# A cross-attention kernel on one core: query weights kept in DRAM, values loaded for two quads, and some transfers issued by GpSimd

## The chip, the cores and the metric

One of the eight cores of a Trainium2 chip runs the kernel. The metric is device time in microseconds (us). The engines are TensorE (PE in the profile, its weight loads PEld), VectorE (DVE), ScalarE (ACT), GpSimd (POOL) and SyncE (SP). In the kernel before, SyncE issues all transfers but two small ones of ScalarE, which load gamma and beta.

## The reference

```python
mu  = jnp.mean(hidden_states, axis=-1, keepdims=True)
var = jnp.var(hidden_states, axis=-1, keepdims=True)
x = (hidden_states - mu) * jax.lax.rsqrt(var + LN_EPS) * ln_gamma + ln_beta
Q = _split_heads(x @ Wq.T)                # 32 heads of 32
K = _split_heads(memory_keys); V = _split_heads(memory_values)
scores = jnp.einsum('bhsd,bhtd->bhst', Q, K) * scale
probs = jax.nn.softmax(jnp.where(mask, scores, -jnp.inf), axis=-1)
attn = jnp.einsum('bhst,bhtd->bhsd', probs, V)     # back to (B, S, 1024)
out = residual + attn @ Wout.T
```

There are 8 batches, 256 queries and 256 keys each, 1024 features, all in fp32. Keys and values are the same input, ctx_4096.

## The kernel before, in words

The unit of work is a quad: four heads of one batch. There are 64 quads, eight to a batch, and the main loop (line 926) has one slot for each, n = 0 to 63. The order of the instructions on each engine is written out by hand, there is no scheduler, and each engine takes its instructions strictly in that order. A wait at the head of a queue holds everything behind it.

In slot n TensorE does: the scores of quad n+1 (`scores`, line 486), the product of the probabilities of quad n-2 with its values (`values`, line 629), a share of a query projection (`make_q`, line 345, for the first three batches; `query_product`, line 447, after that), and some steps of the output projection of the batch before (`product_steps`, line 715). At which place of the slot these steps stand is a table of three counts for each slot of a batch: place 0 is behind the scores, place 1 behind the values, place 2 at the slot's end (`STEPS`, line 662). The program's matmul on fp32 shows as two rows of the trace.

The other engines do the softmax of quad n+1 in slot n (`softmax_parts`). For each head VectorE adds the mask and takes the extreme (line 522), ScalarE takes the exponential with its sum (526), VectorE inverts the sum (533), GpSimd multiplies by it (535, `normalize`), VectorE transposes 32x32 blocks into the tile `pT` (541), and ScalarE copies half of it aside into `pc` (547). Then the tail of the quad: two transfers move parts of `pT` inside `pT` (607), two more bring `pc` into `pT` (611), the second pair waiting for the first to land. For quads below 8, and for those near the end, the tail is put off into the next slot, behind its first exponentials. `ahead` are loads that stand in front of the tail, `between` are loads between its two pairs of transfers.

Both projections use Strassen-Winograd products from batch 3 on (queries) and in the output projection (the last batch has an order of its own), seven products in place of eight. They need sums of weight blocks: B11, B12, B21, B22 are the quarters, T1 to T4 sums of them. GpSimd forms them in slots 3 to 14 for the output weights (`sum_wo`, line 185) and in slots 9 to 22 for the query weights (`sum_wq`, line 398). Before that GpSimd multiplies gamma into the query weights (`fold`, line 366), one of eight chunks at the end of each of the slots 0 to 7. The query sums do not all fit in the on-chip memory: T1 and T3 lie in DRAM (`kept`), and each batch loads them in turn into one tile, `ring` (`load_ring`, line 414); B11 and T4 stay on the chip. The query tile of TensorE has one PSUM buffer of the pool `ps_q`, which ScalarE (`copy_q`, lines 352 to 358) has to empty before TensorE starts the next query product.

The inputs of a batch go through a layer norm: `load_x`, then statistics and the norm (lines 231 to 257), VectorE's block transposes (316), and sixteen small transfers (`move_x`, line 332), which stand in SyncE's queue as four, six and six behind the tails of three slots. The values of a quad are loaded by `load_v` (line 144) in slot n, for use in slot n+2, into one of two buffers of a quad each. The output of a batch is added to the residual by VectorE and GpSimd and stored by SyncE (`store`, line 758, right behind VectorE's addition; `send`, line 744).

Of the kernel before, what the change touches and what calls it, by code (L numbers as in the profile page):

```python
# [46 lines left out]
F32 = mybir.dt.float32  # L47
# [12 lines left out]
def xattn_kernel(  # L60
# [30 lines left out]
    rp = ctx.enter_context(tc.tile_pool(name="rp", bufs=4))  # L91
    lnp = ctx.enter_context(tc.tile_pool(name="lnp", bufs=2))
    kp = ctx.enter_context(tc.tile_pool(name="kp", bufs=2))
    vp = ctx.enter_context(tc.tile_pool(name="vp", bufs=2))
    atp = ctx.enter_context(tc.tile_pool(name="atp", bufs=3))
    ep = ctx.enter_context(tc.tile_pool(name="ep", bufs=4))
    ptp = ctx.enter_context(tc.tile_pool(name="ptp", bufs=3))
    asp = ctx.enter_context(tc.tile_pool(name="asp", bufs=2))
# [24 lines left out]
    xs, ks, vs, rs = {}, {}, {}, {}  # L123

    def load_x(b, s, h=None):

        if b not in xs:
            xs[b] = xp.tile([P, NS, D], F32, tag="x", name=f"x_{b}")
        cols = ds(0, D) if h is None else ts(h, 512)
        nc.sync.dma_start(xs[b][:, s, cols], x[b, ts(s, P), cols])  # L130

    def load_k(n):
# [3 lines left out]
        nc.sync.dma_start(  # L136
            ks[n], kv[b, g // 2, :, : 2 * T].rearrange("p (g t) -> p g t", g=2)
        )

    def load_v(n):  # L140

        b, g = divmod(n, NQ)
        vs[n] = vp.tile([P, NI, P], F32, tag="v", name=f"v_{n}")
        nc.sync.dma_start(
            vs[n],
            kv[b, g // 2, :, ds(2 * T + n % 2 * NI * P, NI * P)].rearrange("p (i v) -> p i v", i=NI),
        )

    def load_res(b, s, h):
        rs[b, s, h] = rp.tile([P, 512], F32, tag="r", name=f"r_{b}_{s}_{h}")  # L150
        nc.sync.dma_start(rs[b, s, h], x[b, ts(s, P), ts(h, 512)])
# [9 lines left out]
        for name in ("T1", "T3")  # L161
    }
    w_t4 = const.tile([P, NK, NK, P], F32, tag="t4", name="t4")
# [7 lines left out]
    def load_wo(which, pair):  # L171
# [3 lines left out]
        nc.sync.dma_start(  # L175
            wo[:, which, ts(pair, 2)], rows.rearrange("(c p) q -> p c q", c=2)
        )

    def sum_wo(which, c):
# [5 lines left out]
        nc.gpsimd.tensor_tensor(wo[:, which, c], wo[:, a, c], wo[:, b, c], op)  # L185
# [24 lines left out]
    load_v(1)  # L210
    for o in range(5, 8):
        load_wq(o)
    for which, pair in ((B12, 0), (B22, 0), (B11, 0), (B12, 1), (B22, 1), (B11, 1)):
        load_wo(which, pair)
# [106 lines left out]
    def move_x(b, part):  # L321
# [8 lines left out]
        for i in part:  # L330
            a, q = i % NA, (i + i // NA) % NA
            nc.sync.dma_start(to_move[b][ts(q, K), a], xes[b][ts(a, K), q])
# [31 lines left out]
    def fold(o):  # L364

        nc.gpsimd.tensor_tensor(
# [11 lines left out]
    SPLIT = 3  # L378
    SOON, LATE = 0, NK
    W_AT = {"B12": (SOON, 0), "B22": (SOON, NK), "B11": (LATE, 0), "B21": (LATE, NK),  # L380
            "T2": (SOON, 0), "T3": (SOON, 0)}

    def weights(name, o):
# [3 lines left out]
        if name == "T4":  # L387
            return w_t4[:, o]
# [3 lines left out]
    def sum_wq(to, o):  # L392
# [5 lines left out]
        nc.gpsimd.tensor_tensor(weights(to, o), weights(a, o), weights(b, o), op)  # L398
# [739 lines left out]
```

## Time and profile before

| what | value |
|---|---|
| time, three runs | 577.17, 577.49, 578.33 us; median 577.49 us |
| profiled execution, first to last instruction (its span) | 577.0 us; no other time is recorded for it |
| the median over that span | 0.49 us |
| TensorE busy, matmuls | 567.3 us, 98% |
| VectorE, ScalarE, GpSimd busy | 460.4, 411.7, 409.8 us (80%, 71%, 71%) |
| DMA traffic | 111.69 MB, mean 194 GB/s |

A row of a timeline or of the groups names line, engine and operation, then the tile written and the tiles read. "Idle before" in brackets is time that the engine stood still just before the row, and what ended it. A row of SPq is the issuing of a transfer by SyncE, not the transfer. PEclk is the TensorE clock granted, as a share of full speed.

### The profile page before, as it was taken

How to read it: one execution, taken by the hardware profiler on the slowest of the kernel's cores; microseconds unless marked ns; L12 is line 12 of the kernel's file. 1: busy time of each engine (PE TensorE's matmuls, PEld its weight loads, DVE VectorE, ACT ScalarE, POOL GpSimd, SP SyncE). 2: the span in 40 equal slices, each digit the busy share in tenths (PEclk: the TensorE clock that was granted, in tenths of full speed). 3: DMA queues.
4: the chain of work that ended last, by engine and by line, in shares of the span. 5: the costliest groups of instructions: out<-in, count | busy, mean ns of one | idle time of the engine just before them, and what ended most of it. 6: DMA issues, size and time to landing. Idle time of an engine off the chain costs nothing. (4 is left out here: it accounts for less than half of the span.)

```text
span 577.0 us, 20128 instructions
## 1 busy us (share of the span) xinstructions
PE 567.3 (98%) x7162; PEld 394.2 (68%) x7162; DVE 460.4 (80%) x1695; ACT 411.7 (71%) x1425; POOL 409.8 (71%) x677
## 2 busy tenths in 40 slices
PE   8999998999999999999999999999999999999997
PEld 8788784667667777677676677667766767755543
DVE  5888887788877879979888788988878878779823
ACT  4697886677667877688677867768767776769810
POOL 1778898889896896876568675676658657448770
PEclk9999999899999999999999999999999999999999
DMA  8974766656677777957678856687567864446751
GB/s 304 394 206 126 208 161 180 192 148 166 185 220 222 200 208 207 271 166 201 188 213 228 211 138 189 212 240 206 148 161 236 224 170 130 130 138 178 199 166 73
DMA packets 50100, 111.69 MB, mean 194 GB/s; under 512 B 9424, under 2 KB 10192, under 8 KB 50000
## 3 DMA queue, kind: packets, MB, share of 16 engines
q1 hardware_dynamic: 49712, 110.40, 66.8%
q8 instruction: 57, 0.93, 0.7%
q14 instruction: 43, 0.35, 0.2%
q10 hardware_dynamic: 288, 0.01, 0.0%
HBM read 60.04 MB, written 10.49 MB: 122 GB/s over the span
## 5 line engine op out<-in xcount | busy, mean ns | idle before, releaser
L535 POOL TENSOR_SCALAR e<-e,rden 128x256 f32<-128x256 f32 x512 | 236.0, 478 | 116.9 <-DVE rden L533 114.4
L526 ACT ACTIVATE e<-e,mn 128x256 f32<-128x256 f32 x512 | 253.9, 501 | 50.7 <-DVE mn L522 49.6
L541 DVE STREAM_TRANSPOSE pT<-e 128x512 f32<-128x512 f32 x256 | 180.9, 707 | 44.7 <-POOL e L535 32.7
L522 DVE CUSTOM_DVE_ANT_0 e<-sc,mb 128x256 f32<-128x256 f32 x512 | 185.4, 416 | 26.4 <-PE sc L486 26.0
L547 ACT COPY pc<-pT 128x512 f32<-128x512 f32 x128 | 79.0, 617 | 72.1 <-DVE pT L541 36.6
L526 ACT ACTIVATION_READ_ACCUMULATOR e<-e,mn 128x1 f32 x512 | 97.9, 191 | 0.0
L345 PE MATMUL pq<-xnT,wq 128*128 128x256 f32 (+1 forms) x368 | 84.1, 383 | 0.6 <-ACT qa L354 0.6
L345 PEld LDWEIGHTS pq<-xnT,wq 128*128 128x128 f32 x368 | 68.9, 190 | 15.4 <-issue 3.7
L629 PE MATMUL pv<-pT,v 64*32 64x128 f32 x4096 | 74.7, 274 | 3.5 <-DMA v<-in_kv_dram 2.9
L629 PEld LDWEIGHTS pv<-pT,v 64*32 64x32 f32 x4096 | 57.5, 105 | 26.7 <-issue 14.7
L486 PEld LDWEIGHTS sc<-k,qa 32*128 32x128 f32 x1024 | 46.2, 184 | 41.9 <-issue 23.6
L715 PE MATMUL po_S<-wo,at 128*128 128x512 f32 x152 | 74.3, 606 | 0.0
L486 PE MATMUL sc<-k,qa 32*128 32x256 f32 x1024 | 73.6, 401 | 0.1
L715 PE MATMUL po_A<-wo,at 128*128 128x512 f32 x128 | 61.2, 620 | 0.3 <-ACT qa L354 0.3
L715 PE MATMUL po_S<-wo,s 128*128 128x512 f32 x104 | 49.9, 606 | 0.0
L533 DVE RECIPROCAL rden<-den 128x2 f32<-128x2 f32 x256 | 37.6, 147 | 7.7 <-ACT e L526 6.8
L522 DVE DVE_READ_ACCUMULATOR2_ANT mn<- 128x1 f32 x512 | 42.5, 83 | 0.0
L715 PEld LDWEIGHTS po_A<-wo,at 128*128 128x128 f32 x128 | 23.4, 193 | 26.2 <-issue 24.5
L447 PEld LDWEIGHTS pq_A<-xnT,wq 128*128 128x128 f32 x320 | 37.3, 192 | 4.8 <-issue 3.6
L715 PEld LDWEIGHTS po_S<-wo,at 128*128 128x128 f32 x152 | 25.8, 190 | 19.7 <-issue 19.1
L447 PE MATMUL pq_A<-xnT,wq 128*128 128x128 f32 x320 | 37.3, 275 | 0.0
L748 POOL TENSOR_TENSOR r<-r,p 128x512 f32<-128x512 f32 x23 | 29.4, 1278 | 7.1 <-DMA r<-in_x_dram 3.3
(96 smaller groups left out, 608.7 us busy)
## 6 DMA issues: line engine op xcount, KB each, us to landing
v<-in_kv_dram SPq DMA_DIRECT2D x64, 256.0 KB, 3.9
pT<-pT SPq DMA_DIRECT2D x128, 128.0 KB, 3.1
pT<-pc SPq DMA_DIRECT2D x128, 128.0 KB, 3.5
ring<-kept_T SPq DMA_DIRECT2D x18, 512.0 KB, 5.2
k<-in_kv_dram SPq DMA_DIRECT2D x32, 256.0 KB, 3.1
x<-in_x_dram SPq DMA_DIRECT2D x14, 512.0 KB, 5.1
r<-in_x_dram SPq DMA_DIRECT2D x28, 256.0 KB, 5.1
out_dram<-r SPq DMA_DIRECT2D x28, 256.0 KB, 3.0
```

The costliest lines, as they stand in the source:

```text
L345: nc.tensor.matmul(pqs[n], wq[:, o, c, :], xnTs[b](c), start=(c == 0), stop=(c == NC - 1),)
L447: nc.tensor.matmul(pqs[b][:, o, :], w[:, c], x_[:, c], start=begins and o + c == 0, stop=c == NK - 1, skip_group_check=True,)
L486: nc.tensor.matmul(scs[n][j][:, s, :], qa[r, n % NQ, ts(s, P)], ks[n - n % 2][r, n % 2, :], start=True, stop=True,)
L522: nc.vector.tensor_tensor_reduce(out=e[:, s, :], in0=pss[j][:, s, :], in1=mbs[n // NQ], scale=1.0, scalar=NO_SCORE, op0=ALU.add, op1=ALU.m ...
L526: nc.scalar.activation(e[:, s, :], e[:, s, :], AF.Exp, bias=mn[:, s : s + 1], scale=-1.0, accum_out=den[:, s : s + 1],)
L533: nc.vector.reciprocal(rden, dens[j])
L535: nc.gpsimd.tensor_scalar(es[j][:, s, :], es[j][:, s, :], rden[:, s : s + 1], 1.0, ALU.mult, ALU.mult,)
L541: nc.vector.transpose(pT[:, :, :, j, :, :].rearrange("p a i s k -> p (a i) s k"), es[j].rearrange("p s (b t) -> p b s t", t=K),)
L547: nc.scalar.copy(pc[:, :, ts(j, 2)], pT[:, 1, :, ts(j, 2)])
L629: nc.tensor.matmul(pvs[n][r][j * HD : (j + 1) * HD], vs[n][ts(r, 2 * K), i, ts(j, HD)], pT[ts(r, 2 * K), :, i, j, :, :], start=(i == 0), s ...
L715: nc.tensor.matmul(po, operand(b, name)[:, c], wo[:, which, c], start=begins and c == 0, stop=c == NK - 1, skip_group_check=not begins,)
L748: nc.gpsimd.tensor_tensor(r, r, p1s[b], ALU.add)
```

## The change

It replaces fixed lists by a table, `PLAN`, and adds choices of engine and slot. What differs in the built program, engine by engine:

- TensorE has the same 3615 matmuls. The third query product (B11) reads `ring`, for batches 4 to 7, and T4 lies where B11 lay in `wq`; its own tile `w_t4` is gone. The output products of batches 0 and 2 to 5 are spread otherwise over the slots, and in batches 0 and 2 the first output tile is added up in two steps and stored a slot later.
- B11 is written to DRAM once (two transfers) and loaded into `ring` for each of batches 4 to 7 (eight transfers of 512 KB), between T1 and T3.
- Values are loaded for two quads at once, 32 loads of 512 KB in place of 64 of 256 KB, for 19 of these pairs a slot sooner than the even quad's own.
- Of the six loads of output weights that stand ahead of the loop, five go to slots 1 to 3 (B21 stays in 3 and 4).
- 36 transfers are issued by GpSimd: 19 output stores, 7 of the small moves of x, 3 loads of x, 4 loads of `ring`, 1 residual load, 1 write of B11, and one `pT<-pc` of quad 4. Most stand at the end of a slot (`at_end`); that of quad 4 stands in front of the first `normalize` of quad 5. The small moves are spread as 7, 4 and 5 over three slots from batch 4 on.
- 27 of the 256 normalisations of a head (54 instructions) go from GpSimd to ScalarE, from L535 to an activation with a scale.
- VectorE takes over 9 of the 32 weight sums from GpSimd, the norm of the second half of batch 1 from GpSimd, and that of the second half of batch 2 from ScalarE. GpSimd takes over the norm of the first half of batch 2, in slot 2.
- `fold` of chunk 0 stands before the loop, the others in slots 1, 3, 3, 4, 5, 6, 7. `asp`, the pool of `pc`, has three buffers instead of two.

The core of the diff:

```diff
+PLAN = {'wq': [[9, 'T1', 0, 'P'], [14, 'T1', 1, 'V'], [15, 'T1', 3, 'V'], [16, 'T3', 2, 'V'], ...
+ 'wo': [[6, 4, 1, 'V'], [13, 3, 1, 'P'], [4, 5, 1, 'P'], [3, 5, 2, 'P'], [4, 5, 0, 'P'], ...
+ 'keeps': [[15, 'T1', 0], [16, 'T1', 1], [17, 'T3', 0], [19, 'T3', 1], [11, 'B11', 0], [13, 'B11', 1]],
+ 'scaled': [[40, 1, 'A'], [9, 2, 'A'], [12, 2, 'A'], [15, 2, 'A'], [49, 2, 'A'], [6, 0, 'A'], [6, 2, 'A'], ...
+ 'norm2': 'PV',
+ 'rings': [[-3, -4], [0, 0], [2, 2]],
+ 'foldat': [-1, 1, 3, 3, 4, 5, 6, 7],
+ 'st0': [0, 0, 0, 0, 6, 1, 0, 1, 1, 0, 3, 3, 0, 1, 0, 0, 1, 1, 0, 2, 1, 0, 3, 0, 0, 4, 0],
+ 'stg': [0, 0, 0, 0, 4, 4, 0, 0, 4, 0, 0, 1, 0, 3, 0, 0, 0, 3, 0, 1, 4, 0, 0, 0, 0, 4, 0],
+ 'woload': [[0, 0, 3], [3, 1, 1], [3, 0, -1], [0, 1, 1], [2, 0, 2], [2, 1, 2]],
+ 'n11': 'V',
+ 'qp': {'sB04': 3, 'out00': 2, 'out01': 2, 'out10': 2, 'out11': 2, 'ringT30': 2, 'mv3_9': 2, 'mv15': 1, 'x1None': 2, ...},
+ 'vearly': {'30': 'z', '44': 'b', '54': 'a', '8': 'a', '10': 'b', '48': 'a', ...},
...
+    def issue(key, to, of):
+        mode = QP.get(key, 0)
+        if mode == 2 and key[0] == 'r' and key[:2] != 'ri':
+            mode = 1
+        if mode == 0 or not in_loop:
+            nc.sync.dma_start(to, of)
+        elif mode == 1:
+            nc.gpsimd.dma_start(to, of)
+        else:
+            at_end.append(partial(nc.gpsimd.dma_start, to, of))
...
-        vs[n] = vp.tile([P, NI, P], F32, tag="v", name=f"v_{n}")
-        nc.sync.dma_start(
-            vs[n],
-            kv[b, g // 2, :, ds(2 * T + n % 2 * NI * P, NI * P)].rearrange("p (i v) -> p i v", i=NI),
-        )
+            vs[n] = vp.tile([P, 2, NI, P], F32, tag="v", name=f"v_{n}")
+        of = kv[b, g // 2, :, 2 * T :].rearrange("p (g i v) -> p g i v", g=2, i=NI)
+            issue(f'v{per(n)}', vs[n], of)
...
-    w_t4 = const.tile([P, NK, NK, P], F32, tag="t4", name="t4")
-            "T2": (SOON, 0), "T3": (SOON, 0)}
+            "T2": (SOON, 0), "T3": (SOON, 0), "T4": (LATE, 0)}
-        ("S1", "ring", True), ("S4", "B22", False), ("A11", "B11", True), ("S2", "T2", False),
+        ("S1", "ring", True), ("S4", "B22", False), ("A11", "ring", True), ("S2", "T2", False),
...
+            for one in [x for x in nexts if x[0] == j]:
+                one[1]()
+                nexts.remove(one)
             rden = sm.tile([P, NS], F32, tag="rden", name=f"rden_{n}_{j}")
             nc.vector.reciprocal(rden, dens[j])
+            engine = SCALED_BY.get((n, j), nc.gpsimd)
             for s in range(NS):
-                nc.gpsimd.tensor_scalar(
+                if engine is nc.scalar:
+                    engine.activation(es[j][:, s, :], es[j][:, s, :], AF.Copy, scale=rden[:, s : s + 1])
+                    continue
+                engine.tensor_scalar(
...
+                if mode == 0:
+                    nc.sync.dma_start(to, of)
+                elif mode == 1:
+                    nc.gpsimd.dma_start(to, of)
+                elif mode == 2:
+                    at_end.append(partial(nc.gpsimd.dma_start, to, of))
+                else:
+                    nexts.append((mode - 3, partial(nc.gpsimd.dma_start, to, of)))
...
-        ahead = [partial(load_v, n)] if n > 1 else []
+        ahead = [partial(load_v, n)] if n > 1 and (n % 2 == 0 or n < VSPLIT) and n not in V_EARLY and str(n) not in V_LATE else []
+        if n + 1 in V_EARLY and V_EARLY[n + 1] == "a":
+            ahead.append(partial(load_v, n + 1))
+        if n + 1 in V_EARLY and V_EARLY[n + 1] == "b":
+            between.append(partial(load_v, n + 1))
...
+        for which, pair, slot in WO_LOADS:
+            if n == slot:
+                between.append(partial(load_wo, which, pair))
...
+        while at_end:
+            at_end.pop(0)()
```

328 lines of the change are left out of this document (254 added, 74 removed), and 12 rows, old and new, of the table PLAN.

## The prediction

> **What bounds the kernel now.** I read the page's first lines, the waits of TensorE, its timeline, the granted clock by stretch, and then, for each wait, the queue that came last.
>
> ```profile
> span 577.0 us, 20128 instructions
> PE 567.3 (98%) x7162; PEld 394.2 (68%) x7162; DVE 460.4 (80%) x1695; ACT 411.7 (71%) x1425; POOL 409.8 (71%) x677
> 61.40 5.42 PE L345 MATMUL pq<-xnT,wq 128*128 128x256 f32 x24 [0.57 <-ACT qa L354]
> 91.11 1.26 PE L629 MATMUL pv<-pT,v 64*32 64x128 f32 x64 [0.55 <-DMA pT<-pT]
> 92.63 5.42 PE L715 MATMUL po_A<-wo,at 128*128 128x512 f32 x12 [0.27 <-ACT qa L354]
> 101.18 1.25 PE L629 MATMUL pv<-pT,v 64*32 64x128 f32 x64 [2.05 <-DMA v<-in_kv_dram]
> 102.36 3.68 PE L715 MATMUL po_A<-wo,at 128*128 128x512 f32 x4
> 363.42 1.98 PE L715 MATMUL po_S<-wo,at 128*128 128x512 f32 x4
> 370.90 1.26 PE L629 MATMUL pv<-pT,v 64*32 64x128 f32 x64 [0.85 <-DMA v<-in_kv_dram]
> 550.83 1.98 PE L782 MATMUL po_end<-wo,at 128*128 128x512 f32 x4 [0.35 <-ACT at L642]
> 102.00:106.00 4.00, 4.00 (x35) 1.74 (x19) 3.18 (x19) 3.15 (x13) 3.51 (x4) 0.57 0.83 236
> ```
>
> TensorE is the bound: 98% busy. Between its first real matmul and its last it stands still six times, 4.64 us in all: 0.57, 0.55, 0.27, 2.05, 0.85, 0.35. One loss more hides in busy time: behind the 2.05 the granted clock is 0.57 over 4 us, and four matmul rows take 3.68 us there against 1.98 elsewhere: 1.70 us. So at most 6.3 us of waiting can be saved. Everything else is a matter of matmuls, whose number the change leaves alone.
>
> **Where the waits come from.**
>
> ```profile
> 53.38 2.37 ACT L252 ACTIVATE x<-x,shift,rstd 128x1024 f32<-128x1024 f32 x2 [1.17 <-POOL shift L249]
> 57.04 0.93 POOL L535 TENSOR_SCALAR e<-e,rden 128x256 f32<-128x256 f32 x2 [0.36 <-DVE rden L533]
> 57.27 1.14 SPq L607 DMA_DIRECT2D pT<-pT  x2
> 83.56 0.45 SPq L130 DMA_DIRECT2D x<-in_x_dram  x1
> 85.97 1.16 SPq L607 DMA_DIRECT2D pT<-pT  x2
> 87.17 0.57 SPq L130 DMA_DIRECT2D x<-in_x_dram  x1
> 92.20 1.71 SPq L611 DMA_DIRECT2D pT<-pc  x2
> 93.96 3.75 SPq L332 DMA_DIRECT2D xnT<-xe  x6
> 97.81 0.53 SPq L144 DMA_DIRECT2D v<-in_kv_dram  x1
> 361.65 5.03 SPq L332 DMA_DIRECT2D xnT<-xe  x6
> 366.77 0.53 SPq L758 DMA_DIRECT2D out_dram<-r  x1
> 367.39 0.41 SPq L144 DMA_DIRECT2D v<-in_kv_dram  x1
> ```
>
> Before the 0.57 at 61.4, ScalarE did both norms of batch 2 in one stretch, 2.37 us, and its query copy came late. The 0.55 and the 0.27 behind it: two loads of x of 512 KB (83.56, 87.17) stand around the pair of moves issued at 85.97; that pair lands late, so SyncE's next pair goes out at 92.20 only. The 2.05 follows in the same queue: behind 92.20 come six moves of x (3.75 us of issuing) and only then, at 97.81, the values, which TensorE wanted at 101.18 - 2.05 = 99.1. At 370 it is again six moves (5.03), a store and then the values.
>
> **The change, part by part.** The sum is made against the span of 577.0 us; the median of the three runs is 577.49, so 0.49 is added at the end. Rows for the length of a slot, for a transfer of 512 KB (the last column is issue to landing) and for the load of the engines:
>
> ```profile
> 378.36 1.08 PE sc L486 x16
> 379.44 1.09 PE pv L629 x64
> 381.58 3.57 PE pq_S L447 x32
> 385.15 1.72 PE po_S L715 x4
> ring<-kept_T SPq DMA_DIRECT2D x18, 512.0 KB, 5.2
> 60.00:80.00 20.00, 19.43 (x280) 15.92 (x260) 18.09 (x73) 16.73 (x61) 18.94 (x28) 1.00 0.70 196
> ```
>
> *Values, loaded by pairs and earlier.* The product at 101.18 is quad 8's. Its values were asked for in slot 8, behind the tail and the six moves of slot 7. Now the pair of quads 8 and 9 is asked for in slot 7, in the queue ahead of the moves issued at 85.97. A load of 512 KB has as its nearest row another of that size, 5.2 us (ring), so it lands at about 91, 8 us before it is wanted. An odd quad's values come with the even one's, a slot sooner than before, and 19 pairs are asked for a slot sooner still. A pair's buffer is free behind the product of an odd quad, about 2 us into the slot; SyncE comes to it later than that, so the moves queued behind the load do not wait for it. Both value waits go: 2.05 + 0.85. Late next would be the `pT` moves of the same quad, which had landed in both places.
>
> *The clock.* It fell only behind the 2.05; the 0.85 left it alone. With the wait gone, 1.70 goes too. The Trainium skill, in "TensorE: Matmul & The Clock Gate" (What's actually happening), says that the clock is either half or full and falls after an idle window of some 3.4 us. The half clock agrees with the 0.57 over 4 us, but here 2.05 us with smaller waits ahead of it was enough; going by that rule alone the 1.70 would have another cause and stay, and the result would be 573.5 instead of the forecast.
>
> *Layer norm of batches 1 and 2.* Rows for the operations that move:
>
> ```profile
> L257 POOL TENSOR_SCALAR x<-x,mv,rstd 128x1024 f32<-128x1024 f32 x1 | 3.8, 3781 | 0.0
> L257 DVE TENSOR_SCALAR x<-x,mv,rstd 128x1024 f32<-128x1024 f32 x3 | 2.4, 803 | 0.1
> L366 POOL TENSOR_TENSOR wq<-wq,gs 128x1024 f32<-128x1024 f32 x8 | 15.2, 1900 | 0.1
> L185 POOL TENSOR_TENSOR wo<-wo 128x512 f32<-128x512 f32 x16 | 20.3, 1276 | 0.0
> L535 POOL TENSOR_SCALAR e<-e,rden 128x256 f32<-128x256 f32 x512 | 236.0, 478 | 116.9 <-DVE rden L533 114.4
> L526 ACT ACTIVATE e<-e,mn 128x256 f32<-128x256 f32 x512 | 253.9, 501 | 50.7 <-DVE mn L522 49.6
> L753 DVE TENSOR_TENSOR r<-po_S,r 128x512 f32<-128x512 f32 x12 | 8.3, 690 | 1.8 <-PE po_S L715 1.2
> pT<-pT SPq DMA_DIRECT2D x128, 128.0 KB, 3.1
> out_dram<-r SPq DMA_DIRECT2D x28, 256.0 KB, 3.0
> ```
>
> ScalarE loses its 2.37 us in slot 3, so the 0.57 goes. GpSimd takes one half, 3.78, in slot 2, where the chunk of `fold` (1.90) no longer stands: 1.9 more there; in exchange the 3.78 of batch 1 leave it before slot 0 for 0.80 on VectorE. The loads of x for batch 3 stand in slots 5 and 7 instead of 6 and 7, which spreads the transfers in front of 85.97: 0.55 and 0.27 go.
>
> *Normalisations and weight sums.* 54 normalisations leave GpSimd (54 x 0.478 = 25.8 us) and come to ScalarE, which has no such row; the nearest is the exponential on the same tile, 0.50, so 27 us, one or two pairs in a slot. Nine sums leave GpSimd (9 x 1.28 = 11.5) for VectorE at 0.69 (6.2). A slot of TensorE here is scores, values and 24 query rows: 1.08 + 1.09 + 5.42 = 7.6 us. ScalarE, busy 16.73 of 20, had 6.4 us of work in it. In slot 5, the tightest, two pairs add 2.0: 8.4, so it ends 0.8 late and puts the query copy back; the neighbours have one pair (7.4) or none. I take 0.3 us of new wait, between 0 and 0.8, nearer to nothing because the norm's 2.37 in slot 3 cost only 0.57.
>
> *GpSimd's transfers.* 36 issues, none of which the trace shows on this engine. Lower bound: below nothing for SyncE, which is freed of 36 x 0.57; on GpSimd at least nothing. Upper bound: GpSimd stands until the transfer has landed, 3.0 us for a store, 5.2 for a ring half. I take the length of SyncE's issue, 0.53 to 0.57, since both only write down what is to be moved: 36 x 0.57 = 20 us, less than the 25.8 + 11.5 that leave. In slots 2 to 10, nine slots of 7.6 us where GpSimd was busy 18.94 of 20, twelve normalisations (5.7) and one sum (1.3) leave and the norm (3.8) comes: 3.2 us less, and four issues, 2.3. Nothing on TensorE's path. The one in slot 4 waits for a landing (3.1): ScalarE comes to its copy 2.37 us before 57.27, at 54.9, so GpSimd's first normalisation starts at about 58.0 instead of 57.04, with three heads instead of four. No wait.
>
> *B11 through DRAM.* Ten transfers of 512 KB more, 5.2 MB on 111.7. A load waits for the product before it and lands in 5.2 us; its product is at least one slot away (B11: two slots). T3 comes later than before, two slots ahead of use. No wait. T4 in `wq` is read the same way.
>
> *Output steps.* Slots of TensorE become uneven. A slot with no step is 1.08 + 1.09 + 3.57 = 5.7 us, the one ahead of it with five steps (ten rows at 0.43) 10.0. VectorE, busy 18.09 of 20 in slots of 7.6, has some 7 us of work in a slot, so it falls behind by 1.3 in the short one, more where statistics fall into it, and has the next slot, with four steps 9.2 us, to recover; the next scores need only the first half of its work. No wait, though the cover is thinner than before.
>
> *The end.* The 0.35 at 550.83 hangs on the last quad's softmax, which is not touched; two stores by GpSimd stand in front of its last sums.
>
> ```profile
> 553.43 0.73 POOL L774 TENSOR_TENSOR ring<-at,at 128x256 f32<-128x256 f32 x1
> 557.37 1.88 PE L782 MATMUL po_end_s<-wo,ring 128*128 128x512 f32 x4
> ```
>
> The sum wanted at 557.37 is ready at 554.2; two issues of 0.57 leave 2 us of room, and two of 3.0 would be late by 2.8.
>
> **Sum.** 2.05 + 0.85 + 1.70 + 0.57 + 0.55 + 0.27 = 5.99 saved, 0.3 new: 577.0 - 5.7 = 571.3 for the span, 571.8 as a median.
>
> **Rivals.** *Part of the waits stays* (0.22). In the first 120 us VectorE and GpSimd are busy 18 to 19 of 20 us and TensorE may only hand its wait on to them. Only the value waits and the clock go, and a wait like 0.57 comes twice: 577.49 - 4.60 + 1.1 = 574.0. (A clock that falls all the same, 573.5, is counted here, 0.03.) Against it: GpSimd's load falls there.
>
> *The early waits come back in full* (0.08): whatever is first late there closes the clock again, and only the 0.85 at 370 is gained: 576.6.
>
> *GpSimd becomes the bound* (0.15, slower). Place: the end of a slot, where its issues stand in front of the next quad's first normalisation. With an issue of 0.8 us the 3.2 us saved in slots 2 to 10 are used up; GpSimd's idle time there was 1.06 of 20, 3.6 in nine slots, so from (3.2 + 3.6) / 4 = 1.7 us on it has more work than TensorE. At 3.0, the landing of a store, four issues make 12.0 - 6.8 = 5.2 us of waiting and 1.70 of clock; later one wait of 0.85 in each of five batches, 4.3: 577.49 - 5.99 + 11.2 = 582.7. For it: no row prices these issues. Against: SyncE's take 0.57. The Trainium skill, in "SBUF — State Buffer" (SBUF: two separate sides), has a rule of this direction: descriptors of GpSimd's transfers are written by that engine and stand still while certain VectorE operations hold a shared port. No run here shows it.
>
> *ScalarE's new work makes query copies late and a wait long enough to close the clock* (0.07, slower by a little): two waits of 2.05 with 1.70 each, 7.5 for 6.0 saved: 579.0. It decides from a ScalarE lateness of about 2 us in one slot, where I count 0.8.
>
> That the change does not do what it says is ruled out by the order of the built program: same matmuls, value loads ahead of the moves.
>
> **How the numbers follow.** Forecast 0.48. A measurement of this kernel can tell 0.2%, 1.15 us. Faster: forecast and first rival, 0.70; same: the second, 0.08; slower: the last two, 0.22. Low end: all 6.34 us of waiting gone and nothing new, 571.15, less most of the 1.16 us by which the three runs differ: 570.2. High end: 579.5, which leaves out about half of the slower cases.
>
> **What would show it.** Right: TensorE's list of waits without the value rows, PEclk 1.00 from 10 to 570 us, four output rows nowhere above 2 us, SyncE's values landing a slot before use. Wrong: rows of GpSimd's normalisation with idle time ended by its own queue, query matmuls waiting for ScalarE with more than 1 us in all, or any stretch with a granted clock of 0.5 to 0.9.

## The result, and the profile after

| kernel | median, us | runs | ratio, 95% interval |
|---|---|---|---|
| before | 577.20 (574.46 to 579.32) | 20 | |
| after | 579.80 (578.41 to 581.49) | 20 | 1.0047 [1.0033, 1.0062] |

The changed kernel is slower by 2.6 us, where 5.7 us less were forecast. All its 20 runs lie above the median of the kernel before. Its profiled execution took 579.36 us, 577.5 of them span. In every run of every kernel whose span is recorded, 1.7 to 1.9 us lie outside the span. So the execution on which the prediction was built, with its span of 577.0, took about 578.8 us, and the typical execution of the kernel before has a span of about 575.4; both are estimates from the 1.8 us.

The page and TensorE's timeline of the changed kernel; the bracket at the end of a row is the idle time before it and what ended it:

```profile
span 577.5 us, 19967 instructions
PE 568.4 (98%) x7162; PEld 395.1 (68%) x7162; DVE 470.9 (82%) x1706; ACT 430.0 (74%) x1477; POOL 397.5 (69%) x648
PEclk9999999999999999999999999999999999999999
60.72 5.42 PE L453 MATMUL pq<-xnT,wq 128*128 128x256 f32 x24 [0.34 <-ACT qa L462]
66.07 2.32 PE L594 MATMUL sc<-k,qa 32*128 32x256 f32 x16
77.98 5.42 PE L453 MATMUL pq<-xnT,wq 128*128 128x256 f32 x24 [0.50 <-POOL e L654]
83.33 2.05 PE L594 MATMUL sc<-k,qa 32*128 32x256 f32 x16
89.25 3.72 PE L453 MATMUL pq<-xnT,wq 128*128 128x256 f32 x16 [0.86 <-POOL wq L474]
92.90 1.15 PE L594 MATMUL sc<-k,qa 32*128 32x256 f32 x16
219.94 3.84 PE L555 MATMUL pq_A<-xnT,wq 128*128 128x128 f32 x32 [0.42 <-DVE wq L504]
224.45 1.98 PE L868 MATMUL po_S<-wo,at 128*128 128x512 f32 x4 [0.67 <-DVE r L910]
244.77 1.26 PE L778 MATMUL pv<-pT,v 64*32 64x128 f32 x64 [0.39 <-PE sc L594]
373.01 7.13 PE L868 MATMUL po_A<-wo,at 128*128 128x512 f32 x16 [0.38 <-DVE qa L571]
```

What was to go has gone: no value product waits for its values, and the clock is full in every slice. In its place stand waits that name GpSimd and VectorE. Part of them hide in rows that are merely longer: the sixteen score matmuls take 2.32 and 2.05 us at 66 and 83, against 1.15 at 92.90. So the busy time of TensorE did not fall by the 1.70 us of clock loss that it held before, but rose by 1.1 us.

Two places show where the new waits begin. The first is the end of slot 3 and slot 4, in the timelines of GpSimd and VectorE, with the answer for the line of the norm (minimum, median and maximum of its length in ns):

```profile
52.09 4.20 POOL L474 TENSOR_TENSOR wq<-wq,gs 128x1024 f32<-128x1024 f32 x2
52.16 2.38 DVE L365 TENSOR_SCALAR x<-x,mv,rstd 128x1024 f32<-128x1024 f32 x1 [0.69 <-POOL rstd L347]
L365 DVE TENSOR_SCALAR x<-x,mv,rstd x5: 790/799/2376, 6.5 to 52.2; 128x1024 f32<-128x1024 f32 x5
54.97 0.51 ACT L638 ACTIVATE e<-e,mn 128x256 f32<-128x256 f32 x1 [3.76 <-DVE mn L634]
59.60 0.74 POOL L645 DMA_DIRECT2D pT<-pc  x1 [1.73 <-DMA pT<-pT]
60.40 1.84 POOL L654 TENSOR_SCALAR e<-e,rden 128x256 f32<-128x256 f32 x4
```

VectorE's norm, new in this place, took 2.38 us beside GpSimd's two chunks of `fold`; the median of its five rows is 0.80. ScalarE idled 3.76 us for the maxima that VectorE had not formed, the tail of quad 4 went out late, and GpSimd waited at the head of its queue for that tail's first move to land, so that its normalisations began at 60.40. Which of the two, the norm or the transfer in GpSimd's queue, makes the score rows long is told by e1 to e3 below.

The second place is the end of slot 22, where the mask for batch 3 is formed:

```profile
215.42 0.58 POOL L213 DMA_DIRECT2D xnT<-xe  x1
216.02 1.28 POOL L844 TENSOR_TENSOR at<-at 128x512 f32<-128x512 f32 x1
216.35 2.34 DVE L584 TENSOR_SCALAR mb<-mk 128x256 f32<-128x256 uint8 x1
217.25 1.28 POOL L504 TENSOR_TENSOR wq<-wq 128x512 f32<-128x512 f32 x1
218.61 1.28 DVE L504 TENSOR_TENSOR wq<-wq 128x512 f32<-128x512 f32 x2
```

VectorE forms a mask for each batch (`mb<-mk`); in the kernel before the longest of the eight took 0.72 us. Here it took 2.34, and it ended when GpSimd's two additions were over; behind it VectorE had two sums of `wq` as new work, and TensorE's waits at 219.94 and 224.45 follow.

### The profile page after: what moved, and what is told of

The parts are those of the page before. It is cut to its first block, busy times and chain, and to the rows that moved or that the text cites. A ratio compares the mean times of both kernels' runs of the same rounds, so it can differ in the third digit from the quotient of the medians.

```text
span 577.5 us, 19967 instructions
## 1 busy us (share of the span) xinstructions
PE 568.4 (98%) x7162; PEld 395.1 (68%) x7162; DVE 470.9 (82%) x1706; ACT 430.0 (74%) x1477; POOL 397.5 (69%) x648
## 4 chain that ended last, share of the span: by engine, by line
PE 64%; DVE 10%; POOL 8%; ACT 6%; DMA 5%; issue 4%; SPq 2%; DVEq 0%; POOLq 0%; ACTq 0%
PE po_S L868 13%; PE pq_A L555 12%; PE po_A L868 9%; PE sc L594 8%; PE pv L778 7%; POOL e L654 6%; PE pq_S L555 5%; PE pq L453 4%; DVE e L634 3%; DMA pT<-pT 3%; ACT e L638 3%; DVE pT L660 3%; PE po_end L935 2%; ACT e L652 1%; SPq L211 1%
## 5 line engine op out<-in xcount | busy, mean ns | idle before, releaser
L654 POOL TENSOR_SCALAR e<-e,rden 128x256 f32<-128x256 f32 x458 | 212.4, 481 | 133.9 <-DVE rden L648 127.2
L634 DVE CUSTOM_DVE_ANT_0 e<-sc,mb 128x256 f32<-128x256 f32 x512 | 185.1, 415 | 17.8 <-PE sc L594 17.8
L594 PE MATMUL sc<-k,qa 32*128 32x256 f32 x1024 | 76.2, 401 | 0.2
L868 PE MATMUL po_S<-wo,at 128*128 128x512 f32 x152 | 73.1, 607 | 0.7 <-DVE r L910 0.7
L594 PEld LDWEIGHTS sc<-k,qa 32*128 32x128 f32 x1024 | 47.6, 184 | 37.7 <-issue 16.8
L868 PE MATMUL po_A<-wo,at 128*128 128x512 f32 x128 | 58.5, 602 | 0.6 <-DVE qa L571 0.4
L868 PE MATMUL po_S<-wo,s 128*128 128x512 f32 x104 | 47.9, 597 | 0.0
L555 PEld LDWEIGHTS pq_A<-xnT,wq 128*128 128x128 f32 x352 | 40.6, 192 | 4.9 <-issue 2.5
L555 PE MATMUL pq_A<-xnT,wq 128*128 128x128 f32 x352 | 41.6, 276 | 0.4 <-DVE wq L504 0.4
L791 ACT COPY at<-pv 128x128 f32<-128x128 f32 x128 | 26.2, 253 | 8.7 <-PE pv L778 8.7
```

Source lines behind the costliest of these rows:

```text
L555: nc.tensor.matmul(pqs[b][:, o, :], w[:, c], x_[:, c], start=begins and o + c == 0, stop=c == NK - 1, skip_group_check=True,)
L594: nc.tensor.matmul(scs[n][j][:, s, :], qa[r, n % NQ, ts(s, P)], ks[n - n % 2][r, n % 2, :], start=True, stop=True,)
L634: nc.vector.tensor_tensor_reduce(out=e[:, s, :], in0=pss[j][:, s, :], in1=mbs[n // NQ], scale=1.0, scalar=NO_SCORE, op0=ALU.add, op1=ALU.m ...
L654: engine.tensor_scalar(es[j][:, s, :], es[j][:, s, :], rden[:, s : s + 1], 1.0, ALU.mult, ALU.mult,)
L791: nc.scalar.copy(ats[b, k][:, c, :, ts(r, 2), :], pv.rearrange("p a s k -> p s a k"))
L868: nc.tensor.matmul(po, operand(b, name)[:, c], wo[:, which, c], start=begins and c == 0, stop=c == NK - 1, skip_group_check=not begins,)
```

## The experiments

Theory 1: GpSimd's transfers cost time, by what they do to VectorE. Theory 2: VectorE's new work does. Rival of both: the structure (512 KB value loads, B11 through DRAM) costs. Eighteen kernels were run, each against the kernel before on the same chip; ratios are to that kernel (its medians lay between 575.5 and 576.9 us).

**All transfers back on SyncE.**

```diff
- 'qp': {'sB04': 3, 'out00': 2, ...},
+ 'qp': {},
```

> The changed kernel with all its 36 GpSimd transfers issued by SyncE again; nothing else differs. Theory A (a program with a GpSimd queue pays about 1.4 us outside the span, whatever the number of transfers): time minus span falls from 1.83 us to 0.5, and GpSimd no longer stands for quad 4's swap, which is worth about 1 us of the waits between 60 and 90 us: 577.0 to 577.5, ratio 1.000. Theory B (issues on GpSimd are what delays normalisations all along): the waits between 60 and 90 us and those after 200 us go, 573. Rival C (SyncE needs the relief): new waits for moves, slower than 579.8.

Measured: 576.13 us, ratio 1.0002 [0.9986, 1.0019]. The ratio is that of theory A, but not for its reason: the time outside the span stays at 1.8 us, and the profile's span is 573.6 us instead of 577.5. Within the intervals the 36 issues explain the whole 0.45% between changed kernel and kernel before. The rest of the change brought nothing net. The longest of the waits that are left:

```profile
67.95 1.26 PE L778 MATMUL pv<-pT,v 64*32 64x128 f32 x64 [1.08 <-ACT e L638]
87.19 3.72 PE L453 MATMUL pq<-xnT,wq 128*128 128x256 f32 x16 [0.85 <-POOL wq L474]
221.34 1.98 PE L868 MATMUL po_S<-wo,at 128*128 128x512 f32 x4 [0.53 <-DVE r L910]
```

**One piece at a time, on the changed kernel.** The norm of batch 2's second half by ScalarE; the tail transfer of quad 4 by SyncE; and, on the kernel before, one store behind the loop by GpSimd:

```diff
- 'norm2': 'PV',
+ 'norm2': 'PA',            # e2
- 'qp': {'sB04': 3, ...},
+ 'qp': {...},              # e3: without sB04
-    send(B - 2, *ENDS_TO[7])
+    nc.gpsimd.dma_start(...)   # e4: the same store
```

> The changed kernel with the norm of the second half of batch 2 on ScalarE instead of VectorE; GpSimd keeps the first half and all transfers. Theory A (VectorE's norm was held to 2.38 us by GpSimd's two weight chunks of 4.2 us, and with the 0.7 us wait for the deviation before it put back slot 4 by 3 us): exponentials of slot 4 start by 52.5 instead of 54.4, the long score rows at 66 to 84 us shrink by 2 of their 2.5 us, the span falls by about 2.5 us, to 575. Theory B (GpSimd's own lateness from the standing in front of quad 4's swap): nothing much changes, under 0.5 us.

> The changed kernel with the one pT<-pc of quad 4 issued by SyncE again, the other 35 GpSimd transfers stay. Theory B of the run before (GpSimd's standing from 57.9 to 59.6 us for the landing and its issue start the chain): first normalisation of quad 5 at 58.0 instead of 60.4, waits at 66 to 84 us shrink by half or more, 1.5 to 2.5 us off the span. Theory A (VectorE's held norm starts it): about 1 us off at most, the query copy still late at 60.7. Time minus span stays 1.83 in both.

> The kernel before with one single output store (of the last but one batch, behind the loop) issued by GpSimd. Theory A (having a GpSimd queue at all costs outside the span): time minus span grows by about 1.3 us to 1.8, the span stays: 578.5, ratio 1.0023. Rival (the cost outside the span goes with the 36 transfers, or was there before): no change, ratio 1.000.

Measured: e2 578.38 us, 1.0036 [1.0016, 1.0055]; e3 578.30, 1.0036 [1.0017, 1.0055]; e4 576.54, 1.0014 [0.9992, 1.0036]. Each of the first two pieces is worth some 0.6 us, no more than their intervals allow to be told; the larger expectations, 2.5 us for e2 and 1.5 to 2.5 for e3, were missed. The traces still tell the pieces apart. GpSimd's first normalisation of quad 5 in e1, e2 and e3, then the score row of the same slot in e2 and e3:

```profile
57.16 1.83 POOL L654 TENSOR_SCALAR e<-e,rden 128x256 f32<-128x256 f32 x4
59.99 1.84 POOL L654 TENSOR_SCALAR e<-e,rden 128x256 f32<-128x256 f32 x4
58.46 1.85 POOL L653 TENSOR_SCALAR e<-e,rden 128x256 f32<-128x256 f32 x4
65.69 2.30 PE L594 MATMUL sc<-k,qa 32*128 32x256 f32 x16
65.67 1.15 PE L593 MATMUL sc<-k,qa 32*128 32x256 f32 x16
```

Without the norm on VectorE (e2) the score row is as long as in the changed kernel (2.32). With the norm there, held for 2.38 us as in the changed kernel, but quad 4's transfer with SyncE (e3, and e1), it takes 1.15. So the long row at 66 goes with the transfer at which GpSimd stands, not with the norm. (e14 and e17 below have the transfer too, and 1.36 and 1.37.) The long row at 83 needs neither: it is 2.06 in e3 and 2.01 in e16, which has no transfer by GpSimd and no norm of batch 2 on VectorE.

e4's ratio cannot tell its two expectations apart, since both lie in its interval. The time outside the span can: it is 1.79 us with a transfer by GpSimd, as without any. e4 also gives a second look at what is, up to the loop's end, the kernel before:

```profile
92.44 1.25 PE L629 MATMUL pv<-pT,v 64*32 64x128 f32 x64 [2.31 <-DMA pT<-pT]
101.90 1.25 PE L629 MATMUL pv<-pT,v 64*32 64x128 f32 x64 [1.65 <-DMA v<-in_kv_dram]
```

The waits around 90 to 101 are there again, in other sizes, and this time nothing is lost to the clock (it stays at 1.00 from 92 to 108 us), although one wait is longer than the 2.05. In the kernel before the mean granted clock was 0.996 or 0.997 in 34 of 145 runs, and 0.999 or 1.000 in the others: 0.3% of 574 us is 1.7 us. The clock loss that the prediction counted as certain occurs in about one execution of four: in 15 of 35 on one chip, in 19 of 110 on two others.

**Which of GpSimd's transfers.** e9 keeps 27 transfers of the later batches (18 stores, 3 ring loads, 3 moves of x, 3 loads of x); e10 keeps the other nine: the tail transfer of quad 4, four moves of x (not five, as the expectation of e9 counts), a residual load, a store, the write of B11 and one ring load of the last batch.

```diff
- 'qp': {... all 16 kinds ...},
+ 'qp': {out00, out01, out10, out11, ringT30, mv15, x1None},                                     # e9
+ 'qp': {sB04, keptB111, out1_01, mv3_9, mv2_13, mv2_7, r1_01, mv3_2, ring7_B110},               # e10
```

> The changed kernel without those of GpSimd's transfers that stand in the batches 1 to 3 (the pT move of quad 4, three small moves of batch 2, two of batch 3, a residual load, a store of batch 1, the write of B11, one ring load): these go back to SyncE. The stores and ring loads of the later batches stay with GpSimd. Theory, the cost of GpSimd's issuing lies where GpSimd is short of time, in the first 240 us: 1.000 to 1.0015, as with all transfers on SyncE (1.0002). Rival, each issue costs the same wherever it stands: two thirds of 2.5 us stay, 1.003.

> The counterpart of e9_late_gpsimd: only the transfers of batches 1 to 3 stay with GpSimd, stores and ring loads of the later batches go back to SyncE. Theory, the cost lies early: 1.0035 to 1.005, as the changed kernel. Rival, each issue costs the same: 1.001 to 1.002.

Measured: e9 577.12 us, 1.0018 [1.0004, 1.0031]; e10 578.15, 1.0036 [1.0016, 1.0057]. e10 meets its theory, e9 lies between its two. The nine transfers cost about 2.0 us over e1, the twenty-seven about 0.9, where equal shares would be 0.65 and 1.95; the intervals are nearly as wide as these differences. The traces divide in the same way: e10 has the first place of the changed kernel (GpSimd's normalisation at 60.64, score rows of 2.31, 1.61 and 2.05 us) and no mask above 0.72, e9 has the second (a mask of 2.37).

**The structure, on the old slots and engines.** e5 switches back all that can be: three entries of PLAN are left, which set old values. e6 adds the early values, e11 the ring slots, e12 both.

```diff
+PLAN = {'bufs': {'asp': 2}, 'scaled': [], 'rings2': [0, 2]}          # e5
+        'vearly': {...}                                              # e6 and e12
+        'rings': [[-3, -4], [0, 0], [2, 2]]                          # e11 and e12
```

> The changed program with the slots, engines and queues of the kernel before: only what cannot be switched back stays (values loaded for two quads in the even quad's own slot, B11 through DRAM, T4 in B11's place). Theory 1, the structure is free and takes nothing of the wait for quad 8's values, which are asked for in the same slot as before: 0.999 to 1.001 of the kernel before. Rival, the structure itself costs (512 KB land later than 256 KB, ten transfers more): 1.002 or above. Prediction's step on values, read strictly: the value wait of 0.85 at 370 could go for odd quads only, so 0.0 to 0.9 us faster.

> The kernel of e5_tables_old with one more thing: 19 pairs of values asked for a slot sooner, as in the changed kernel. It measures the largest term of the prediction by itself. If the waits for values of the profiled execution (2.05 and 0.85, and the clock loss of 1.70) are those of every execution, 4.6 us go: ratio 0.992. If that execution was an unusually long one and the clock falls in one execution of five only, the median gains 1 to 2.5 us: ratio 0.9955 to 0.998. If the wait is only handed on to the moves of pT, 0.999 to 1.001.

> The kernel of e5_tables_old with the slots of the ring loads of the changed kernel (T1 three and four slots ahead of a batch, B11 both halves in slot 0, T3 both in slot 2, in place of one half a slot). e5_tables_old stood 13.3 us for ring loads, in front of B11's and T3's second products. If those slots hide the ten transfers, as the prediction says of B11 through DRAM, the ring waits go and the kernel stands with the kernel before: 0.999 to 1.001. Rival, the loads take bandwidth from values and moves all the same: 1.003 to 1.010.

> The kernel of e11_rings with 19 pairs of values asked for a slot sooner, and nothing else of the change: the prediction's largest term by itself, now without the ring waits that covered it in e6_values_early. If the profiled execution of the kernel before was typical: 4.6 us, 0.992. If the clock falls in one execution of five and the value waits are shorter on most: 1 to 2.5 us, 0.9955 to 0.998, and then this kernel beats both. If the wait is handed on to the moves of pT: 0.999 to 1.001.

Measured: e5 593.16 us, 1.0277 [1.0245, 1.0310]; e6 594.80, 1.0341 [1.0306, 1.0376]; e11 579.44, 1.0037 [1.0009, 1.0064]; e12 573.80, 0.9962 [0.9941, 0.9984]. For e5 only the rival's "1.002 or above" holds, and those for e6 all miss: they left out that ring loads of one half a slot come too late. In the list of waits (total us, times, longest) e5 has

```profile
PE pq_A L479 <- DMA ring<-kept_T: 10.8, 4, 3.9
PE pq_A L479 <- DMA ring<-kept_B: 2.5, 3, 1.5
```

and the ring slots of e11 take them away. What e11 still stands above the kernel before, 0.37% or 2.1 us, is in the range of e11's rival; its trace shows waits of up to 2.36 us (at 102.58, behind `pc`), none of which names a ring. Values a slot sooner then bring 0.75%, 4.3 us, between e11 and e12, on one chip (the clock loss showed in 8 of e11's 12 runs and in 2 of e12's). Against the kernel before, from whose waits the prediction took its 2.05, 0.85 and 1.70, e12 gains 0.38%, 2.2 us, as its second expectation said. What is left of TensorE's waits inside the loop of e12:

```profile
90.56 5.42 PE L814 MATMUL po_A<-wo,at 128*128 128x512 f32 x12 [0.23 <-ACT qa L408]
113.42 1.12 PE L814 MATMUL po_S<-wo,at 128*128 128x512 f32 x2 [0.67 <-DVE r L852]
147.48 1.98 PE L814 MATMUL po_S<-wo,at 128*128 128x512 f32 x4 [0.24 <-DVE r L856]
```

**VectorE's and ScalarE's new work, with all transfers on SyncE.** e7 gives the 54 normalisations back to GpSimd, e16 only batch 2's second norm to ScalarE, e8 that norm and three sums.

```diff
- 'scaled': [[40, 1, 'A'], ...],
+ 'scaled': [],                                            # e7
- 'norm2': 'PV',
+ 'norm2': 'PA',                                           # e8, e16
- [22, 'T4', 2, 'V'], [22, 'T4', 0, 'V'], [6, 4, 1, 'V']
+ [22, 'T4', 2, 'P'], [22, 'T4', 0, 'P'], [6, 4, 1, 'P']   # e8
```

> The kernel of e1_all_sync (no transfers by GpSimd) with all normalisations back on GpSimd: what ScalarE's 54 new instructions cost or gain where GpSimd has no issues to do. Prediction's step, ScalarE late by at most 0.8 us in slot 5, 0.3 us of wait: 0.9995 times e1_all_sync. Rival, with the norm in slot 2 and two folds at the end of slot 3 GpSimd has no room and the normalisations are needed on ScalarE: 1.002 to 1.004 times e1_all_sync.

> The kernel of e1_all_sync with three of VectorE's new pieces of work taken from it again: the norm of the second half of batch 2 goes to ScalarE, the two sums of T4 in slot 22 and the sum of slot 6 to GpSimd. In e1_all_sync TensorE still waits 0.8 us behind a fold (86.0), 0.5 behind an output addition of VectorE (220.5) and 0.4 (368.7). Theory, VectorE held by its new work is what makes these late: the first two go, 1 us, 0.9985. Rival, the work is only handed back: 1.000 or above, with waits for wq at 75 to 90 and 220.

> The kernel of e1_all_sync (1.0002) with one of the three moves of e8_sync_eased (0.9952): the norm of the second half of batch 2 by ScalarE in place of VectorE. If that norm, which stood for 2.38 us instead of 0.80 behind GpSimd's two folds, is what puts VectorE back in slots 3 to 6: most of the 2.9 us, 0.996 to 0.9975. If the sums (slots 6 and 22) matter more: 0.999.

Measured: e7 575.96 us, 0.9985 [0.9966, 1.0004]; e8 574.07, 0.9952 [0.9930, 0.9973]; e16 575.26, 0.9979 [0.9963, 0.9995]. Against e1's 1.0002 the three pieces of VectorE's work are worth 0.5%, 2.9 us, nearly half of it the norm, and more than the 1 us that e8's theory expected. Theory 2 holds. The 54 normalisations make no difference that these intervals can tell.

**GpSimd's transfers on kernels with room.** e14 is e8, and e15 is e12 (with the third buffer for the copies aside), both with the 36 transfers.

```diff
- 'qp': {},
+ 'qp': {... all 16 kinds ...},
```

> The changed kernel, GpSimd's 36 transfers included, with three of VectorE's new pieces of work taken from it (as in e8_sync_eased, which is this kernel with all transfers on SyncE and stands at 0.9952). If GpSimd's transfers cost their 2.5 us whatever VectorE does: 0.9995 to 1.000. If they cost only because VectorE had no room left to make good a late GpSimd: 0.996 to 0.9975.

> The kernel of e12_rings_values (0.9962) with the 36 transfers of the changed kernel issued by GpSimd (and its third buffer for the copies aside), on the tables of the kernel before: the price of these issues where GpSimd also has all its sums and normalisations. Prediction's step, 0.57 us each and hidden: 0.996 to 0.9975. By the pair of changed kernel and e1_all_sync: plus 2.6 us, 1.0005 to 1.001. If they use up the room of GpSimd, busy 18.9 of 20 us in slots 2 to 10 here: above 1.002.

Measured: e14 579.15 us, 1.0043 [1.0022, 1.0064]; e15 580.33, 1.0067 [1.0042, 1.0092]. By the ratios (the pairs stood on different chips) the issues cost 5.2 us over e8 and 6.0 over e12, more than in the changed kernel; of the expectations only e15's last holds. For that one, GpSimd's room used up, e15's trace has a place: GpSimd is busy 29.16 of the 30 us from 120 on, and TensorE waits 1.20 us for one of its sums at 147.91. The end of slot 22 in e14, by its timelines:

```profile
214.91 0.58 POOL L212 DMA_DIRECT2D xnT<-xe  x1
215.51 1.28 POOL L843 TENSOR_TENSOR at<-at 128x512 f32<-128x512 f32 x1
215.84 4.78 DVE L583 TENSOR_SCALAR mb<-mk 128x256 f32<-128x256 uint8 x1
216.74 3.72 POOL L503 TENSOR_TENSOR wq<-wq 128x512 f32<-128x512 f32 x3
225.41 1.99 PE L867 MATMUL po_S<-wo,at 128*128 128x512 f32 x4 [2.28 <-DVE r L909]
```

The mask takes 4.78 us: it stands from 0.33 us behind the start of GpSimd's first addition until the last of the four is over.

**The one issue in front of it.** e17 takes the kind of move at 214.91 out of e14's GpSimd queue; e18 puts nothing but it into e12.

```diff
- 'qp': {..., 'mv15': 1, ...}
+ 'qp': {...}               # e17: e14 without mv15
+ 'qp': {'mv15': 1}         # e18: e12 with it alone
```

> The kernel of e14_eased_gpsimd (1.0043) with one kind of GpSimd's transfers given back to SyncE: the small move of x that stands behind GpSimd's normalisations in one slot of each of the batches 4 to 7. In e14_eased_gpsimd it is issued at 214.91 (0.58 us), GpSimd's four additions follow at 215.51 to 220.46, and VectorE's mask bias, begun at 215.84, takes 4.78 us instead of 0.72. Theory, an issue costs by shifting GpSimd's additions onto an operation of VectorE that cannot run beside them: the mask row is back at about 0.7, the wait of 2.28 at 225 goes, ratio 1.000 to 1.0015. Rival, the late mask has another reason or GpSimd's issue holds VectorE by itself: row and wait stay, 1.004.

> The kernel of e12_rings_values (0.9962), all transfers on SyncE, with only that one small move of x for each of the batches 4 to 7 issued by GpSimd: four issues of 0.58 us in the whole kernel. In e12_rings_values GpSimd's addition begins at 212.24 and the mask bias at 212.94 takes 0.72. Theory: the addition begins 0.58 us later, the mask bias falls at its start and stands until GpSimd's run of additions is over, 2.3 to 3.5 us, and TensorE waits 1 to 2.3 us behind it at about 219: ratio 0.998 to 1.0005. Rival, four issues cost four times 0.58 at most, and hidden: 0.996 to 0.997.

Measured: e17 575.95 us, 1.0010 [0.9990, 1.0029], 0.33% below e14; e18 576.94, 1.0017 [1.0001, 1.0034], 0.55% above e12, 3.2 us for three issues (the table names this move for batches 4 to 7, but the last batch has keys of its own, so three are issued). First e12, then e18, by the timelines of GpSimd, VectorE and TensorE and the clock by stretch (PEclk is the third number from the end):

```profile
212.24 1.27 POOL L790 TENSOR_TENSOR at<-at 128x512 f32<-128x512 f32 x1
212.94 0.72 DVE L530 TENSOR_SCALAR mb<-mk 128x256 f32<-128x256 uint8 x1
213.47 2.57 POOL L450 TENSOR_TENSOR wq<-wq 128x512 f32<-128x512 f32 x2
```

```profile
212.16 0.74 POOL L160 DMA_DIRECT2D xnT<-xe  x1
212.88 3.93 DVE L531 TENSOR_SCALAR mb<-mk 128x256 f32<-128x256 uint8 x1
212.93 1.29 POOL L791 TENSOR_TENSOR at<-at 128x512 f32<-128x512 f32 x1
214.17 2.48 POOL L451 TENSOR_TENSOR wq<-wq 128x512 f32<-128x512 f32 x2
221.59 3.06 PE L815 MATMUL po_S<-wo,at 128*128 128x512 f32 x4 [2.45 <-DVE r L857]
221.00:225.00 4.00, 3.41 (x8) 1.25 (x12) 3.40 (x8) 3.12 (x10) 1.96 (x5) 0.67 0.97 242
```

GpSimd's additions come 0.69 us later, VectorE's mask takes 3.93 us instead of 0.72, TensorE stands 2.45 us, and the clock falls behind it (in 7 of e18's 12 runs, in 2 of e12's, on another chip). The two other issues also lengthen a mask, to 1.12 and 1.13 us from 0.51, but no wait of TensorE follows. In e17's profile the longest mask is 0.725 us again and the wait of 2.28 has shrunk to 0.25. This part of the cost is shown by taking the issue out and by putting it in; e18's ratio lies even above its theory's range. It is not the whole: e17, with 33 transfers left to GpSimd, still stands 0.58%, 3.3 us, above e8.

**A faster version.** e13 is e12 with batch 0's output steps and the later first store of the changed kernel.

```diff
+        'st0': [0, 0, 0, 0, 6, 1, ...], 'p1late': [0]
```

> The kernel of e12_rings_values with batch 0's output steps and its later first store as in the changed kernel. In e12_rings_values TensorE's longest wait left is 0.8 us at 112.4, behind VectorE's addition of the first output tile, and 0.4 at 146.9. If the uneven steps with the store a slot later are what hides the first: 0.7 to 1.2 us below e12_rings_values, ratio to the kernel before 0.994 to 0.9955. Rival, slots of uneven length put VectorE back and another wait comes in: 0.9962 or above.

Measured: 573.52 us, 0.9948 [0.9929, 0.9966], the lowest median of all, 3.35 us below the kernel before on the same chip (576.87) and well below the changed kernel. The wait at 113.4 is gone, others of up to 0.77 us came at other places; against e12 and e8 the difference cannot be told.

## Why the prediction was wrong, point by point

- **The sum's base: wrong.** 0.49 us was added for what lies outside the span; it is 1.8. The profiled execution was longer than the median by about 1.6 us, and the waits counted from it (6.34 us) are not the median's. By the same steps the forecast should have been 571.3 + 1.8, about 573, and 1.70 of the saving was there in about one execution of four only.
- **Values by pairs: right in kind, too large.** Both waits went. Together with the clock they were to bring 4.6 us over the kernel before; with all of the structure that they need (e12) 2.2 are left. The 4.3 between e11 and e12 is counted from e11, which had lost 2.1 first.
- **The clock: right that a wait can cost twice, wrong to count on it.** It fell behind waits of 2.05 (before) and 2.45 us (e18), and behind one of 1.90 (e9, granted clock 0.63 from 68 to 72 us). It stayed full behind 2.31 (e4) and 2.28 (e14). So the length of the wait alone does not decide. Of the rule quoted in the prediction from the Trainium skill, "TensorE: Matmul & The Clock Gate" (What's actually happening), the half clock agrees (the granted clock is 0.51 from 102.4 to 105 us in the kernel before) and the idle window of some 3.4 us does not: these gaps were shorter, and enough.
- **Layer norm: the term was mis-sized, and a neighbour was missed.** 0.80 us on VectorE was read from rows that stood beside no large operation of GpSimd (from 6.10 to 19.51 in the kernel before). At its new place it stands beside `fold` and took 2.38. The 0.57 shrank to 0.34. With all transfers on SyncE the norm's place is worth 0.23%, 1.3 us (e16 against e1), and the wait of 1.08 at 67.95 of e1 is gone without it; the long score row at 66 is not its work (e2, e3). GpSimd's two chunks in one slot were counted as work, not as a neighbour.
- **ScalarE's normalisations: not contradicted.** 0.3 us was allowed, e7 shows no difference that can be told.
- **Sums by VectorE: right in length, wrong in place.** Two sums took 1.28 us, 0.64 each for the 0.69 assumed. They stand behind the mask at the end of slot 22, where VectorE had no room; e8, without them, has no wait at 220. With the norm they cost 2.9 us (e8 against e1), which the prediction put at nothing.
- **GpSimd's transfers: this step failed.** An issue of 0.57 us was right (0.58 at 215.42, 0.74 at 59.60; between e1 and the changed kernel GpSimd's busy time grows by 20.9 us for 36), and so was the room in GpSimd's queue: it was busy 397.5 us, 12 less than before. "Nothing on TensorE's path" does not follow: the issues cost 2.6 us here (e1), and 5 to 6 on e8 and e12. It took an engine with room for an engine whose times do not matter. Two ways in which they matter are seen. The issue of a move shifts GpSimd's additions onto VectorE's mask, which then stands beside them: shown by e17 and e18. And GpSimd stands at quad 4's transfer: the prediction had it start at 58.0 behind it, it started at 60.40, because the landing it waits for was itself late; the traces of e1 to e3 show it, the times can hardly tell it.
- **B11 through DRAM: right only with the new ring slots.** e5 shows 13.3 us of waits for ring loads without them, e11 none, and none is left in the changed kernel's profile; but the cover is thin, since e16's profile, with the same slots, has one of 1.18 us. The reason given, one slot being more than a landing of 5.2 us, is not what hides it: with one half a slot it does not.
- **Output steps and the end: not contradicted.** e13 shows no loss for batch 0; the steps of batches 2 to 5 were not run by themselves. The end's 0.35 stayed (0.36).

Added up by the ratios: of 5.7 us to be saved, structure and early values bring 2.2 (e12), VectorE's new work costs 2.9 (e8 against e1) and GpSimd's transfers 2.6 (e1). The pieces were measured on different kernels, so that their sum, 3.3 us slower, need not be the 2.6 measured.

Of the rivals, "GpSimd becomes the bound" was on the right side, for a wrong reason: in the changed kernel GpSimd was not short of time (at most 17.8 of 20 us in the four stretches from 40 to 120), and no price of 1.7 us for an issue is needed. That price came from the fullest stretch alone: over the 80 us from 40 on, GpSimd was busy 68.8 us in the kernel before, so nine slots held about 9.6 us of its idle time (an estimate) instead of 3.6. In e15 it was short. The rule quoted beside it, from the Trainium skill, "SBUF — State Buffer" (SBUF: two separate sides), also says that a VectorE operation which takes both pairs of ports and an operation of GpSimd exclude each other, and that the one which starts first holds the shared pair for its whole instruction. The traces agree that the two get in each other's way: 0.72 to 2.34, 3.93 and 4.78 for the mask, 0.80 to 2.38 for the norm. Whether the mask and the norm take both pairs of ports no trace says. On the rest rule and traces differ: in e18 the mask's row begins 0.05 us ahead of the addition's and the mask is held all the same, and it stood through two to four operations of GpSimd, not one. The rule would have told which rows to look for. The half that the prediction quoted, descriptors that stand still, was neither needed nor tested.

Open: most of the transfers' cost is shown only as a sum. Of the 2.0 us of e10's nine the tail transfer of quad 4 accounts for 0.6 (e3, within its interval), and for the others there is the timeline but no experiment of its own; nor is there one for the 3.3 us that e17 keeps over e8.

## What to carry to other kernels

A duration belongs to a place: before an operation is moved, look at what the engine that shares something with it does at that time, on both engines, and before a queue gets half a microsecond more, look at what its later work will fall upon. Check the profiled execution against the median through the time outside the span, and count a loss that does not occur in every execution only by its share. Change one table at a time: the part of this change that pays, values a slot sooner and the ring slots, was hidden by two parts that cost more.

## What the runs showed of the hardware that was not expected

- VectorE's mask operation, 0.72 us or less, stood through a whole run of GpSimd's additions in each case seen in which it began within about 0.4 us of the start of the first: 2.34 us for two, 3.93 and 3.49 (e15) for three, 4.78 for four. When it began 0.70 us behind that start (e12, 212.94 against 212.24), or 0.91 (e17, 214.45 against 213.54, below), it came in between the first addition and the next. The norm at 52.16 also came in between two chunks of `fold`. So the wait can last for several operations of GpSimd, and not only for the one that runs; what decides it is not settled.

```profile
213.54 1.28 POOL L842 TENSOR_TENSOR at<-at 128x512 f32<-128x512 f32 x1
214.45 0.52 DVE L582 TENSOR_SCALAR mb<-mk 128x256 f32<-128x256 uint8 x1
214.77 3.80 POOL L502 TENSOR_TENSOR wq<-wq 128x512 f32<-128x512 f32 x3
```

- An issue by GpSimd takes about as long as one by SyncE: for stores in the changed kernel 0.59 us against 0.58 (medians of 19 and 9). Loads of x and small moves land later there: 8.0 and 5.7 us (medians of three and of seven) against 4.6 and 2.5 by SyncE. They stand at other places of the loop, and part of the gap is the place: with all transfers on SyncE (e1) the medians are 6.0 and 3.6. Stores (3.9 against 3.6) and loads of T1 and T3 (4.6 against 5.4) show little or none.

```profile
xnT<-xe SPq DMA_DIRECT2D x89, 64.0 KB, 2.5
xnT<-xe POOLq DMA_DIRECT2D x7, 64.0 KB, 5.7
x<-in_x_dram SPq DMA_DIRECT2D x11, 512.0 KB, 4.6
x<-in_x_dram POOLq DMA_DIRECT2D x3, 512.0 KB, 8.0
```
